# Four graph layers in fp32: a quarter of each symmetric product mirrored by VectorE square transposes and SBUF-to-SBUF transfers instead of TensorE, h^T of layer 3 turned from h, and a new plan

## The chip, the cores and the metric

The kernel runs on one core of one Trainium2 chip. The metric is the device time of one execution in microseconds; the figure that counts is the median of several runs. The engines of the core are TensorE (PE in the profile; its weight loads are listed apart as PEld), VectorE (DVE), ScalarE (ACT) and GpSimd (POOL). SyncE (SP) does no arithmetic here: it issues DMA transfers, one after the other, in the order in which they stand in the program. Everything is computed in fp32.

## What is computed

There are 16 graphs of 1024 nodes with 128 features, and four layers in a row, each of the form x = x + layer(relu(layernorm(x))). The layers that matter here are 0 and 3, which build a 1024 x 1024 symmetric matrix; layers 1 and 2 are given in a line each.

```python
# layer 0, three times (i = 0, 1, 2)
h = h @ W[i] + b[i]
nh = h / max(norm(h), EPS)
cos = einsum('bij,bkj->bik', nh, nh)          # symmetric, 1024 x 1024
h = einsum('bpq,bqc->bpc', adj * cos, h)
h = relu(h)                                    # not after the last one

# layer 1: y = relu(((1 + eps) * h + adj^T h) @ W1 + b1) @ W2 + b2
# layer 2: softmax of tanh(s1 + s2) over the neighbours, times h @ W

# layer 3
h = einsum('bnf,of->bno', x, W_w) + W_b
e = einsum('bil,bkl->bik', h @ A, h)
e = e + swapaxes(e, 1, 2)                      # symmetric, 1024 x 1024
att = softmax(where(adj > 0, e, 0), axis=1) * adj
h_prime = relu(einsum('bij,bjk->bik', att, h))
# then three sigmoid gates from x and h_prime, and a tanh
```

## The kernel before

**Tiles.** A graph is a "batch" in the code. Its 1024 nodes are eight blocks (`NB`) of 128 (`P`), the partitions of the memory. x and h stand as 128 x 1024, block after block along the free dimension. A row j of a square is 128 nodes against all 1024, worked in two halves (`HALVES`, s = 0 and 1) of four blocks[...].

**A square.** `row_of_square` (line 582) makes half a row of the symmetric product in PSUM. Blocks on or above the diagonal are multiplied (L587). Blocks below it are mirrored: the block above the diagonal was copied out of PSUM by ACT in `keep_above` (L609) into a buffer `above` with places for 22 blocks (`PLACE`), and PE transposes it into the row (L597), one instruction per block. There are 36 multiplied and 28 transposed blocks in a square. Of these 28, sixteen are the lower left quarter: rows 4 to 7, half 0. `layer0` has three squares a batch; each half row is multiplied by the norm and the adjacency on DVE (L740, tile `ew`) and then used by PE as an operand of the sum over nodes (`acc`, L620 in the first two, L631 in the third). `layer3` has one: DVE masks the half row (L921, tile `e`), takes the row's maximum (L930), ACT exponentiates (L934), DVE multiplies by the adjacency (L941), and PE accumulates (L620).

**h in layer 3.** Two forms of it are wanted. The transposed one, `hT`, is an operand of the square; before the change it is a product of its own on PE, `ph` (L463, two of 512 columns a batch, beside `pg` for the other operand `gT`), with the bias added by ACT. The plain one, `h`, comes from the products `psP` (L453) and a DVE addition (L909). In it a block is 131 columns wide (`E3`), since three gate columns stand beside each block.

**Loads.** The transposed adjacency of a batch, eight tiles `adjT` of 128 x 1024, is fetched from HBM as 32 x 32 squares put in transposed place, in four transfers a tile (L673), and each square is then turned by DVE (L681) and summed by ACT (L684). The plain rows, `adjL`, come later for layer 1 (L654), and x by L646. All are issued by SP. Sixteen adjT slots are two batches; a slot comes free in layer 3, after L941 of the old tile.

**What sets the order.** The program first lists every operation with a cost in microseconds, what it reads and what it writes, for all batches. `Plan.order` then simulates the five queues (PE, DVE, ACT, POOL, DMA) with these costs and fixed latencies, and places one operation after the other: of those that can start earliest on an engine, the one with the smallest rank. The rank is a due time of the batch (`PERIOD`, `LAST`) less the work that follows, less an entry of the table `LEADS` for its kind ("02 DVE ew" is the kind ew on DVE in the third square of layer 0). Buffers are slots of pools (`POOLS`); `KINDS` limits how many a kind may hold, and how many younger batches may. Operations of up to three batches are mixed. The result is one fixed order for each engine. On the chip each engine, and SP, takes its instructions strictly in this order and waits by semaphores.

Of the kernel before, what the change touches and what calls it, by code (L numbers as in the profile page):

```python
# [14 lines left out]
P = 128  # L15
N = 1024
NB = N // P
D = 128
# [200 lines left out]
def tile_adj_preln(  # L219
# [96 lines left out]
    for load_it in first:  # L316
# [8 lines left out]
    bg = const.tile([D, 1], F32, name="bg")  # L325


    POOLS = {"adjT": 16, "adjL": 4, "x": 3, "big": 16, "above": 2, "bank": 8, "small": 25, "row": 5}
    KINDS = {
        "adjT": ("adjT", 16, 16), "adjL": ("adjL", 4, 4), "x": ("x", 3, 3), "w4": ("big", 13, 13),  # L330
        "chunk": ("big", 12, 4), "above": ("above", 2, 1), "ps": ("bank", 6, 4), "acc": ("bank", 6, 4),
        "small": ("small", 19, 7), "row": ("row", 3, 2),
    }
    PERIOD, LAST, AHEAD, WINDOW = 74.0, 9.0, 2, 0.02

    LEADS = {
        "0 ACT hT": -82.5, "0 ACT hn": 118.5, "0 DVE hn": 4.5, "0 DVE mv": -23.5, "0 DVE nb": -70,
        "0 DVE st": -22.5, "0 PE ps": -2.5, "0 POOL rstd": -10, "00 ACT hT": -39.5, "00 ACT hTn": -130.5,
        "00 ACT sq": -51, "00 DMA params": -55.5, "00 DVE ew": -9.5, "00 DVE h": -17.5, "00 DVE params": 4,
        "00 PE acc0": -148, "00 PE params": -1, "00 PE ps": -43.5, "00 PE psP": -14.5, "00 PE sq": 11.5,  # L340
        "00 POOL rn": 17.5, "01 ACT above": -5, "01 ACT hTn": -2.5, "01 ACT sq": -2.5, "01 DVE ew": 130.5,
        "01 DVE h": 4, "01 DVE ss": 1.5, "01 PE ps": -315, "01 PE psP": 37, "01 PE sq": -2, "01 POOL rn": 0.5,
        "02 ACT above": 9, "02 ACT hTn": 20, "02 ACT sq": -24, "02 DVE ew": 70.5, "02 DVE h": 54,
        "02 DVE ss": -52, "02 DVE x": 50.5, "02 PE acc0": 20.5, "02 PE ps": 6.5, "02 PE psP": 193,
        "02 PE sq": 127.5, "02 POOL rn": 15.5, "1 ACT g": 0.5, "1 ACT y1": 7, "1 DMA adjL": -303.5,
        "1 DVE adjL": -206.5, "1 DVE hn": -5, "1 DVE mv": -39.5, "1 DVE nb": 77.5, "1 DVE st": 8.5,
        "1 DVE x": 89.5, "1 PE acc1": -17.5, "1 PE py": -17, "1 PE py2": 2.5, "1 POOL rstd": -43.5,
        "2 ACT e2": -22, "2 ACT h": -71, "2 ACT hfl": -9, "2 ACT hn": 11.5, "2 ACT hnT": 196, "2 DVE alone": -1,
        "2 DVE e2": 7.5, "2 DVE h": -40, "2 DVE hn": 12.5, "2 DVE hrow": -4.5, "2 DVE mv": 20,
        "2 DVE rden": -64, "2 DVE st": -9.5, "2 DVE x": 101.5, "2 PE p1": -7.5, "2 PE pf": -35.5,  # L350
        "2 PE ps": -227, "2 PE psP": -292, "3 ACT above": -242.5, "3 ACT e3": -38.5, "3 ACT gT": 62.5,
        "3 ACT gate": -13.5, "3 ACT h3T": -65.5, "3 ACT hn": 24, "3 ACT hnT": 18, "3 ACT hp": 17,
        "3 ACT hs": -65.5, "3 DMA z": 17, "3 DVE e3": -116, "3 DVE gate": 6.5, "3 DVE hn": 69, "3 DVE mv": 14.5,
        "3 DVE nb": 254, "3 DVE st": 66, "3 DVE sum": -74, "3 DVE top": 3, "3 DVE z": 29.5, "3 PE acc3": -12,
        "3 PE ph": 198.5, "3 PE ps": 49.5, "3 PE psN": -172.5, "3 PE psP": 6, "3 POOL rstd": 59.5,
        "3 POOL z": -22.5, "T ACT adjT": 127.5, "T DMA adjT": -128.5, "T DVE adjT": -231.5, "x DMA x": 9,
    }
    plan = Plan(POOLS, KINDS, lambda b: min(b * PERIOD, (B - 2) * PERIOD + LAST), AHEAD, WINDOW, LEADS)
    now = [0, ""]
# [7 lines left out]
    def pe(us, reads, writes, fn):  # L367
        return op("PE", us, reads, writes, fn)
# [13 lines left out]
    def ps(name):  # L382
        return Buf("ps", [P, HALF], name)
# [11 lines left out]
        return Buf("row", [P, D], name)  # L395


    MM_BLOCK = 0.222
    MM = 4 * P / 2400
    TR = 0.109  # L400
    TINY = 0.09
    STT = 0.262

# [10 lines left out]
    def blk(b, lo, hi, w=D):  # L414

        return (b, lo * w, hi * w)

    def cols(t, c, w=D):
        return t[:, c * w : c * w + P]

    def span(t, lo, hi):
        return t[:, lo * P : hi * P]
# [12 lines left out]
    def power(dst, src):  # L435
        pool_op(1.64, [src], [dst], lambda: nc.gpsimd.tensor_tensor(dst.t, src.t, mhalf, op=ALU.pow))  # L436

    def flip(src, lo, hi, dst):


        def emit():
            for c in range(lo, hi):
                nc.tensor.transpose(cols(dst.t, c - lo), cols(src.t, c), ident)  # L443

        pe((hi - lo) * TR, [blk(src, lo, hi)], [dst], emit)

    def project(srcT, lo, hi, w, dst):

# [27 lines left out]

        act(S((hi - lo) * P, bias is not None, accum is not None), [src], w, emit)

    def flipped(src, name, func=AF.Copy, accum=None):

        dst = w4(name)
        for s, (lo, hi) in enumerate(HALVES):
            p = ps(f"ps_{name}_{s}")
            flip(src, lo, hi, p)
            evict(p, dst, lo, hi, func, accum=(accum, s) if accum else None)
        return dst

# [82 lines left out]

    PLACE = {(0, 1): 16, (0, 2): 17, (0, 3): 18, (1, 2): 19, (1, 3): 20, (2, 3): 21}
    for r in range(4):
        for c in range(4, NB):
            PLACE[r, c] = r * 4 + c - 4
    PLACE.update({(4, 5): 16, (4, 6): 17, (4, 7): 18, (5, 6): 19, (5, 7): 20, (6, 7): 21})

    def row_of_square(k, j, s, leftT, rightT, above):

        lo, hi = HALVES[s]
        dst = ps(f"sq_{k}_{j}_{s}")
        first = max(lo, j)
        if first < hi:
            pe(
                (hi - first) * MM, [blk(leftT, j, j + 1), blk(rightT, first, hi)], [dst],
                lambda: nc.tensor.matmul(  # L587
                    dst.t[:, (first - lo) * P :], cols(leftT.t, j), span(rightT.t, first, hi), start=True, stop=True
                ),
            )  # L590
        n = min(hi, j) - lo
        if n > 0:
            at = [PLACE[r, j] for r in range(lo, lo + n)]

            def mirrored():
                for r, p in enumerate(at):
                    nc.tensor.transpose(cols(dst.t, r), cols(above.t, p), ident)  # L597

            pe(n * TR, [blk(above, p, p + 1) for p in at], [dst], mirrored)
        return dst  # L600

    def keep_above(dst, j, s, above):
        lo, hi = HALVES[s]
        first = max(lo, j + 1)
        if first < hi:
            p = PLACE[j, first]
            act(
                S((hi - first) * P), [dst], [blk(above, p, p + hi - first)],
                lambda: nc.scalar.copy(span(above.t, p, p + hi - first), dst.t[:, (first - lo) * P :]),  # L609
            )  # L610

    def above_of(k):
        return Buf("above", [P, 22 * P], f"above_{k}")

    def accumulate(acc, h, at, w, ew, j):

# [72 lines left out]
    def layer0(b, xt, aT, prepared):  # L689
# [4 lines left out]
        for i in range(3):  # L694
# [34 lines left out]
            dve(TINY, [ss], [ss], lambda ss=ss: nc.vector.tensor_scalar_max(ss.t, ss.t, NORM_EPS * NORM_EPS))  # L729
            rn = small(f"rn_{k}", NB)  # L730
            power(rn, ss)
            above = above_of(k)
            acc = [bank(f"acc0_{k}_{s}") for s in range(2)]
            for j in range(NB):
                ew = chunk(f"ew_{k}_{j}")
                for s, (lo, hi) in enumerate(HALVES):
                    pc = row_of_square(k, j, s, hTn, hTn, above)
                    o = dve(
                        V(HALF, True), [pc, rn, blk(aT[j], lo, hi)], [blk(ew, lo, hi)],
                        lambda pc=pc, ew=ew, rn=rn, j=j, lo=lo, hi=hi: nc.vector.scalar_tensor_tensor(  # L740
                            span(ew.t, lo, hi), pc.t, rn.t[:, j : j + 1], span(aT[j].t, lo, hi),
                            op0=ALU.mult, op1=ALU.mult,
                        ),
                    )
                    keep_above(pc, j, s, above)
                if prepared is None and j == 3:
                    prepared = prepare(o)
                if i < 2:
                    accumulate(acc, h, j, D, ew, j)
                else:  # L750
                    accumulate_nodes(acc, HALVES, h, j, D, D, ew)
# [137 lines left out]
    def layer3(b, xt, aT):  # L889
# [2 lines left out]
        hn = layernorm(k, xt)  # L892
        hnT = flipped(hn, f"hnT_{k}", AF.Relu)
        relu(hn)
        hT, gT = w4(f"h3T_{b}"), w4(f"gT_{b}")
        for s, (lo, hi) in enumerate(HALVES):
            for dst, w, v, name in ((hT, w3e[:, 0:D], wb3col, "ph"), (gT, wg, bg, "pg")):
                p = ps(f"{name}_{b}_{s}")
                wide(p, w, hnT, lo, hi)
                evict(p, dst, lo, hi, AF.Identity, v)  # L900

        h = w4(f"h_{k}")
        for lo, hi in THIRDS:
# [6 lines left out]
                    by_block(h.t[:, lo * E3 : hi * E3], E3, n), by_block(pp.t, E3, n), per_feature(b3e, n)  # L910
                ),
            )
        above = above_of(k)
        acc = [bank(f"acc3_{b}_{s}") for s in range(2)]
        for j in range(NB):
            e = chunk(f"e3_{b}_{j}")
            for s, (lo, hi) in enumerate(HALVES):
                p = row_of_square(k, j, s, gT, hT, above)
                dve(
                    V(HALF), [blk(aT[j], lo, hi), p], [blk(e, lo, hi)],  # L920
                    lambda e=e, p=p, j=j, lo=lo, hi=hi: nc.vector.scalar_tensor_tensor(  # L921
                        span(e.t, lo, hi), span(aT[j].t, lo, hi), 0.0, p.t, op0=ALU.is_gt, op1=ALU.mult
                    ),
                )
                keep_above(p, j, s, above)
            top = small(f"top_{b}_{j}", 1)
            tot = small(f"sum_{b}_{j}", 1)
            dve(
# [192 lines left out]
```

## Time and profile before

| | |
|---|---|
| median of 3 runs | 2551.03 us (2550.04 to 2552.56) |
| profiled execution: its time | 2549.91 us |
| profiled execution: span of the trace | 2548.1 us |
| mean granted TensorE clock | 0.995 |
| SP queue (q1) | 567552 packets, 142.65 MB, 29.6% of the 16 DMA engines' span |
| PE matmuls L597 (mirrored blocks) | 1792, idle before them 4.9 us |
| DVE L740 (ew) | 768, mean 741 ns |

The profile is of one execution, so sums are made against its 2549.91 us; the trace's span is 1.8 us shorter than that. In rows by line, "busy" is the time that the group kept its engine busy, "mean" is how long one instruction took from start to end, and after the bar stands the idle time of the engine just before them, with what ended it. Instructions of one engine overlap at their ends, so the pitch from one to the next is less than the mean. An engine's idle time costs something only where the chain of work runs through it.

### The profile page before, as it was taken

What the parts mean: (1) busy time and instruction counts of PE and PEld (TensorE: products, weight loads), DVE (VectorE), ACT (ScalarE), POOL (GpSimd) and SP (SyncE); (2) the same over time, 40 slices, a digit from 0 to 9 for tenths busy, and PEclk for the clock granted to TensorE, in tenths of its full rate; (3) what the DMA queues carried; (4) which work ended last, traced back from release to release, by engine and by line L of the source; (5) the groups of instructions that cost most, each with busy time, mean ns of one, the idle gap of its engine ahead of it and who ended that gap; (6) DMA issues with size and microseconds to landing.
All of it is one profiled execution on the core that took longest, in us unless ns stands there. A gap on an engine that the chain in (4) does not pass through costs nothing.

```text
span 2548.1 us, 35510 instructions
## 1 busy us (share of the span) xinstructions
PE 2500.2 (98%) x12714; PEld 1674.1 (66%) x12714; DVE 2003.7 (79%) x5070; ACT 1384.7 (54%) x2609; POOL 215.3 (8%) x134
## 2 busy tenths in 40 slices
PE   7999999999999999999999999999999999999996
PEld 4567576775667666676666767657676666765763
DVE  6658979787787968879687796877878778796777
ACT  4426575644646556455654656447464564554365
POOL 1001000101101010010100101010010100100000
PEclk9999999999999999999999999999999999999998
DMA  9320706133070430604216052340614306042100
GB/s 138 68 67 4 146 1 101 49 52 98 1 124 26 59 91 11 133 7 67 83 26 123 1 84 66 46 104 1 116 34 59 91 8 122 21 59 75 30 12 17
DMA packets 588641, 154.32 MB, mean 61 GB/s; under 512 B 537520, under 2 KB 572080, under 8 KB 588464
## 3 DMA queue, kind: packets, MB, share of 16 engines
q1 hardware_dynamic: 567552, 142.65, 29.6%
q10 hardware_dynamic: 20912, 9.40, 1.4%
q8 instruction: 100, 1.64, 0.3%
q14 instruction: 77, 0.63, 0.1%
HBM read 143.61 MB, written 8.39 MB: 60 GB/s over the span
## 4 chain that ended last, share of the span: by engine, by line
PE 91%; DVE 4%; ACT 2%; DMA 1%; SPq 1%; issue 1%; POOLq 0%; POOL 0%; ACTq 0%; DVEq 0%
PE acc L620 33%; PE acc L631 18%; PE sq L587 17%; PE sq L597 7%; PE psP L453 5%; PE py L463 2%; PE py L792 2%; PE ps_hTn L443 1%; PE ph L463 1%; PE ps_hnT L443 1%; PE pg L463 1%; PE psN L453 1%; SPq L673 1%; DVE e L921 1%; DVE top L930 1%; ACT e L934 1%
## 5 line engine op out<-in xcount | busy, mean ns | idle before, releaser
L740 DVE SCALAR_TENSOR_TENSOR ew<-sq,rn,adjT 128x512 f32<-128x512 f32 x768 | 555.0, 741 | 133.9 <-PE sq L597 84.4
L609 ACT COPY above<-sq 128x512 f32<-128x512 f32 (+3 forms) x640 | 285.2, 455 | 491.6 <-DVE ew L740 431.1
L620 PE MATMUL acc<-ew,h 128*128 128x512 f32 x1024 | 498.4, 597 | 1.6 <-DVE ew L740 1.5
L587 PE MATMUL sq<-hTn 128*128 128x512 f32 (+3 forms) x1152 | 452.2, 489 | 2.4 <-ACT hTn L475 2.4
L597 PEld LDWEIGHTS sq<-ident,above 128*128 128x128 f32 x1792 | 226.5, 141 | 156.9 <-issue 108.3
L597 PE MATMUL sq<-ident,above 128*128 128x128 f32 x1792 | 299.8, 273 | 4.9 <-ACT above L609 4.9
L620 PEld LDWEIGHTS acc<-ew,h 128*128 128x128 f32 x1024 | 177.2, 191 | 147.0 <-issue 100.2
L587 PEld LDWEIGHTS sq<-hTn 128*128 128x128 f32 x1152 | 189.3, 191 | 121.2 <-issue 84.6
L631 PEld LDWEIGHTS acc<-h,ew 128*128 128x128 f32 x2048 | 244.1, 192 | 31.7 <-issue 14.4
L631 PEld LDWEIGHTS acc<-h,e 128*128 128x128 f32 x2048 | 239.9, 193 | 30.3 <-issue 27.1
L631 PE MATMUL acc<-h,ew 128*128 128x128 f32 x2048 | 251.5, 275 | 0.3 <-DVE ew L740 0.3
L631 PE MATMUL acc<-h,e 128*128 128x129 f32 x2048 | 241.1, 276 | 2.5 <-DVE e L862 2.5
L934 ACT ACTIVATE e<-e,top 128x1024 f32<-128x1024 f32 x128 | 146.9, 1148 | 171.9 <-DVE top L930 166.5
L620 PE MATMUL acc<-e,hs 128*128 128x512 f32 x512 | 235.7, 596 | 1.5 <-DVE e L941 1.5
L620 PE MATMUL acc<-adjL,hn 128*128 128x512 f32 x512 | 236.8, 593 | 0.3 <-ACT hn L567 0.2
L862 DVE SCALAR_TENSOR_TENSOR e<-adjT,e 128x512 f32<-128x512 f32 x256 | 165.2, 686 | 64.0 <-ACT e L858 63.8
L436 POOL TENSOR_TENSOR rstd<-ve,mhalf 128x8 f32<-128x8 f32 x64 | 104.8, 1637 | 1096.0 <-DVE ve L528 1092.6
L684 ACT ACTIVATE adjT<-adjT 128x1024 f32<-128x1024 f32 x128 | 135.3, 1057 | 95.5 <-DVE adjT L681 78.5
L921 DVE SCALAR_TENSOR_TENSOR e<-adjT,sq 128x512 f32<-128x512 f32 x256 | 170.5, 675 | 6.5 <-PE sq L587 6.5
L941 DVE TENSOR_TENSOR e<-e,adjT 128x512 f32<-128x512 f32 x256 | 167.3, 679 | 0.0
L681 DVE STREAM_TRANSPOSE adjT<-adjT 128x1024 f32<-128x1024 f32 x128 | 155.8, 1229 | 8.8 <-DMA adjT<-in_adj_dram 4.6
L620 PEld LDWEIGHTS acc<-adjL,hn 128*128 128x128 f32 x512 | 93.8, 190 | 101.4 <-issue 88.6
(121 smaller groups left out, 3260.8 us busy)
## 6 DMA issues: line engine op xcount, KB each, us to landing
adjT<-in_adj_dram SPq DMA_DIRECT2D x512, 128.0 KB, 3.9
adjL<-in_adj_dram SPq DMA_DIRECT2D x128, 512.0 KB, 4.0
x<-in_x_dram SPq DMA_DIRECT2D x16, 512.0 KB, 5.1
out_dram<-z ACTq DMA_DIRECT2D x16, 512.0 KB, 5.6
b<-in_L_gnn_b_dram ACTq DMA_DIRECT2D x4, 64.0 KB, 4.5
w<-in_L_gnn_W_dram ACTq DMA_DIRECT2D x2, 128.0 KB, 3.9
w<-in_L_gnn_W_dram ACTq DMA_DIRECT2D x3, 64.0 KB, 3.5
w2e<-in_L_gnn_W_dram ACTq DMA_DIRECT2D x1, 64.0 KB, 2.7
```

The costliest lines, as they stand in the source:

```text
L453: nc.tensor.matmul(dst.t[:, (c - lo) * n : (c - lo + 1) * n], cols(srcT.t, c), w, start=True, stop=True)
L587: lambda: nc.tensor.matmul(dst.t[:, (first - lo) * P :], cols(leftT.t, j), span(rightT.t, first, hi), start=True, stop=True),
L597: nc.tensor.transpose(cols(dst.t, r), cols(above.t, p), ident)
L609: lambda: nc.scalar.copy(span(above.t, p, p + hi - first), dst.t[:, (first - lo) * P :]),
L620: lambda s=s, lo=lo, hi=hi: nc.tensor.matmul(acc[s].t, cols(h.t, at, w), span(ew.t, lo, hi), start=(j == 0), stop=(j == NB - 1)),
L631: nc.tensor.matmul(a.t[:, (c - lo) * n : (c - lo + 1) * n], cols(ew.t, c), h.t[:, j * w : j * w + n], start=(j == 0 and c == lo), stop=(j ...
L681: dve(V(N), [t], [t], lambda t=t: nc.vector.transpose(t.t, t.t), True)
L740: lambda pc=pc, ew=ew, rn=rn, j=j, lo=lo, hi=hi: nc.vector.scalar_tensor_tensor(span(ew.t, lo, hi), pc.t, rn.t[:, j : j + 1], span(aT[j].t ...
L862: lambda e=e, j=j, lo=lo, hi=hi: nc.vector.scalar_tensor_tensor(span(e.t, lo, hi), span(aT[j].t, lo, hi), 0.0, span(e.t, lo, hi), op0=ALU. ...
L921: lambda e=e, p=p, j=j, lo=lo, hi=hi: nc.vector.scalar_tensor_tensor(span(e.t, lo, hi), span(aT[j].t, lo, hi), 0.0, p.t, op0=ALU.is_gt, op ...
L934: lambda e=e, top=top, tot=tot: nc.scalar.activation(e.t[:, 0:N], e.t[:, 0:N], AF.Exp, bias=top.t, accum_out=tot.t),
L941: lambda e=e, j=j, lo=lo, hi=hi: nc.vector.tensor_mul(span(e.t, lo, hi), span(e.t, lo, hi), span(aT[j].t, lo, hi)),
```

## The change

Three things are changed, and the plan's numbers.

1. In batches 1 to 13 (`FAR`) the lower left quarter of each square is not transposed by PE. When half 1 of rows 0 to 3 has been multiplied, DVE turns each 32 x 32 square of it, from PSUM into `above` (`keep`), where ACT copied it before. After rows 1 and 3, SP sends two rows' worth from `above` to a new buffer `got` (`send`): 16 transfers within SBUF, one for each pair of partition groups of 32, which move the squares to their transposed places, 128 bytes a piece. In rows 4 to 7 the DVE operation (ew in layer 0, the mask in layer 3) reads `got` for half 0 where it read PSUM. There is one `got`. The rest of a square is as before, and batches 0, 14 and 15 keep PE's transposes throughout.
2. In layer 3 of all batches `hT` is turned from `h` by PE transposes (`flipped`, with blocks 131 wide) and copied out by ACT; the product `ph` is gone.
3. `PLACE` is numbered anew.
4. The pools, the limits, the due times, PE's costs and the table `LEADS` are replaced, so that the fixed order of all engines is a new one. There is one more adjL slot, and three fewer of the large buffers.

```diff
-    POOLS = {"adjT": 16, "adjL": 4, "x": 3, "big": 16, "above": 2, "bank": 8, "small": 25, "row": 5}
+    POOLS = {"adjT": 16, "adjL": 5, "x": 3, "big": 13, "above": 2, "got": 1, "bank": 8, "small": 30, "row": 4}
     KINDS = {
-        "adjT": ("adjT", 16, 16), "adjL": ("adjL", 4, 4), "x": ("x", 3, 3), "w4": ("big", 13, 13),
-        "chunk": ("big", 12, 4), "above": ("above", 2, 1), "ps": ("bank", 6, 4), "acc": ("bank", 6, 4),
-        "small": ("small", 19, 7), "row": ("row", 3, 2),
+        "adjT": ("adjT", 16, 16), "adjL": ("adjL", 5, 5), "x": ("x", 3, 3), "w4": ("big", 13, 5),
+        "chunk": ("big", 10, 8), "above": ("above", 2, 1), "got": ("got", 1, 1), "ps": ("bank", 7, 5),
+        "acc": ("bank", 8, 5), "small": ("small", 12, 6), "row": ("row", 2, 2),
     }
-    PERIOD, LAST, AHEAD, WINDOW = 74.0, 9.0, 2, 0.02
+    PERIOD, LAST, AHEAD, WINDOW = 61.0, 2.0, 2, 0.02
 
     LEADS = {
...
     }
...
-    MM_BLOCK = 0.222
-    MM = 4 * P / 2400
-    TR = 0.109
+    MM_BLOCK = 0.2235
+    MM = 0.2155
+    TR = 0.1097
+
+    FAR = range(1, B - 2)
...
-    def flip(src, lo, hi, dst):
+    def flip(src, lo, hi, dst, w=D):
 
 
         def emit():
             for c in range(lo, hi):
-                nc.tensor.transpose(cols(dst.t, c - lo), cols(src.t, c), ident)
-
-        pe((hi - lo) * TR, [blk(src, lo, hi)], [dst], emit)
+                nc.tensor.transpose(cols(dst.t, c - lo), cols(src.t, c, w), ident)
+
+        pe((hi - lo) * TR, [blk(src, lo, hi, w)], [dst], emit)
...
-    def flipped(src, name, func=AF.Copy, accum=None):
+    def flipped(src, name, func=AF.Copy, accum=None, w=D):
...
-            flip(src, lo, hi, p)
+            flip(src, lo, hi, p, w)
...
-    PLACE = {(0, 1): 16, (0, 2): 17, (0, 3): 18, (1, 2): 19, (1, 3): 20, (2, 3): 21}
-    for r in range(4):
-        for c in range(4, NB):
-            PLACE[r, c] = r * 4 + c - 4
-    PLACE.update({(4, 5): 16, (4, 6): 17, (4, 7): 18, (5, 6): 19, (5, 7): 20, (6, 7): 21})
...
-
-        lo, hi = HALVES[s]
-        dst = ps(f"sq_{k}_{j}_{s}")
-        first = max(lo, j)
...
-    def keep_above(dst, j, s, above):
-        lo, hi = HALVES[s]
-        first = max(lo, j + 1)
-        if first < hi:
-            p = PLACE[j, first]
-            act(
-                S((hi - first) * P), [dst], [blk(above, p, p + hi - first)],
-                lambda: nc.scalar.copy(span(above.t, p, p + hi - first), dst.t[:, (first - lo) * P :]),
-            )
...
+    PLACE = {(0, 1): 0, (0, 2): 1, (0, 3): 2, (1, 2): 3, (1, 3): 4, (2, 3): 5}
+    PLACE.update({(r + 4, c + 4): p for (r, c), p in PLACE.items()})
+    PLACE.update({(r, c): 6 + r * 4 + c - 4 for r in range(4) for c in range(4, NB)})
+    QUARTER = NB // 2
+
+    class Square:
+
+
+        def __init__(self, k, leftT, rightT, by_dma):
+            self.k, self.leftT, self.rightT, self.by_dma = k, leftT, rightT, by_dma
+            self.above = Buf("above", [P, 22 * P], f"above_{k}")
+
+            self.got = Buf("got", [P, QUARTER * HALF], f"got_{k}") if by_dma else None
+
+        def row(self, j, s):
+
+            lo, hi = HALVES[s]
+            if self.by_dma and j >= QUARTER and s == 0:
+                q = j - QUARTER
+                return self.got, lambda: self.got.t.rearrange("p (r c d) -> p c r d", r=QUARTER, d=P)[:, q]
+            leftT, rightT, above = self.leftT, self.rightT, self.above
...
+            return dst, lambda: by_block(dst.t, D, 4)
+
+        def keep(self, j, s, read):
+
+            lo, hi = HALVES[s]
+            if self.by_dma and j < QUARTER and s == 1:
+                p, above = PLACE[j, lo], self.above
+                dve(
+                    V(HALF), [read], [blk(above, p, p + 4)],
+                    lambda: nc.vector.transpose(span(above.t, p, p + 4), read.t),
+                )
+                if j % 2:
+                    self.send(j - 1, j + 1)
+                return
+            first = max(lo, j + 1)
+            if first < hi:
+                p, above = PLACE[j, first], self.above
+                act(
+                    S((hi - first) * P), [read], [blk(above, p, p + hi - first)],
+                    lambda: nc.scalar.copy(span(above.t, p, p + hi - first), read.t[:, (first - lo) * P :]),
+                )
+
+        def send(self, lo, hi):
+
+            above, got = self.above, self.got
+            at, end = PLACE[lo, QUARTER], PLACE[hi - 1, NB - 1] + 1
+
+            def squares_to_places():
+                for a in range(P // SQ):
+                    for g in range(P // SQ):
+                        src = span(above.t, at, end)[a * SQ : (a + 1) * SQ]
+                        dst = span(got.t, lo * 4, hi * 4)[g * SQ : (g + 1) * SQ]
+                        with nc.allow_non_contiguous_dma(reason="squares"):
+                            nc.sync.dma_start(
+                                dst.rearrange("p (b a i) -> p b a i", a=P // SQ, i=SQ)[:, :, a],
+                                src.rearrange("p (b g i) -> p b g i", g=P // SQ, i=SQ)[:, :, g],
+                            )
+
+            op("DMA", 1.9 * (hi - lo), [blk(above, at, end)], [blk(got, lo * 4, hi * 4)], squares_to_places)
...
-            above = above_of(k)
+            square = Square(k, hTn, hTn, b in FAR)
...
-                    pc = row_of_square(k, j, s, hTn, hTn, above)
+                    pc, view = square.row(j, s)
...
-                        lambda pc=pc, ew=ew, rn=rn, j=j, lo=lo, hi=hi: nc.vector.scalar_tensor_tensor(
-                            span(ew.t, lo, hi), pc.t, rn.t[:, j : j + 1], span(aT[j].t, lo, hi),
-                            op0=ALU.mult, op1=ALU.mult,
+                        lambda view=view, ew=ew, rn=rn, j=j, lo=lo, hi=hi: nc.vector.scalar_tensor_tensor(
+                            by_block(span(ew.t, lo, hi), D, 4), view(), rn.t[:, j : j + 1],
+                            by_block(span(aT[j].t, lo, hi), D, 4), op0=ALU.mult, op1=ALU.mult,
                         ),
+                        pc is square.got,
                     )
-                    keep_above(pc, j, s, above)
+                    square.keep(j, s, pc)
...
-        hT, gT = w4(f"h3T_{b}"), w4(f"gT_{b}")
+        gT = w4(f"gT_{b}")
         for s, (lo, hi) in enumerate(HALVES):
-            for dst, w, v, name in ((hT, w3e[:, 0:D], wb3col, "ph"), (gT, wg, bg, "pg")):
-                p = ps(f"{name}_{b}_{s}")
-                wide(p, w, hnT, lo, hi)
-                evict(p, dst, lo, hi, AF.Identity, v)
+            p = ps(f"pg_{b}_{s}")
+            wide(p, wg, hnT, lo, hi)
+            evict(p, gT, lo, hi, AF.Identity, bg)
...
-        above = above_of(k)
+        hT = flipped(h, f"h3T_{b}", w=E3)
+        square = Square(k, gT, hT, b in FAR)
...
-                p = row_of_square(k, j, s, gT, hT, above)
+                p, view = square.row(j, s)
                 dve(
                     V(HALF), [blk(aT[j], lo, hi), p], [blk(e, lo, hi)],
-                    lambda e=e, p=p, j=j, lo=lo, hi=hi: nc.vector.scalar_tensor_tensor(
-                        span(e.t, lo, hi), span(aT[j].t, lo, hi), 0.0, p.t, op0=ALU.is_gt, op1=ALU.mult
+                    lambda e=e, view=view, j=j, lo=lo, hi=hi: nc.vector.scalar_tensor_tensor(
+                        by_block(span(e.t, lo, hi), D, 4), by_block(span(aT[j].t, lo, hi), D, 4), 0.0, view(),
+                        op0=ALU.is_gt, op1=ALU.mult,
                     ),
+                    p is square.got,
                 )
-                keep_above(p, j, s, above)
+                square.keep(j, s, p)
```

## The prediction

> **What bounds the kernel now.** I read the page's busy shares first, then the chain that ended last, then a table by stretches over one period of the steady part, then the rows of the operations that the edit touches, and last the sync engine's (SP's) queue in order of time.
>
> ```profile
> PE 2500.2 (98%) x12714; PEld 1674.1 (66%) x12714; DVE 2003.7 (79%) x5070; ACT 1384.7 (54%) x2609; POOL 215.3 (8%) x134
> ...
> PE 91%; DVE 4%; ACT 2%; DMA 1%; SPq 1%; issue 1%; POOLq 0%; POOL 0%; ACTq 0%; DVEq 0%
> ```
>
> TensorE (PE) is busy 98% of the span and carries 91% of the chain that ended last; VectorE (DVE) carries 4%. To see whether that holds within a stage, I took one period. SP's queue in order of time gives it (loads of the transposed adjacency, and of its rows):
>
> ```profile
> 701.25 37.69 SPq L673 DMA_DIRECT2D adjT<-in_adj_dram  x32
> 746.20 20.71 SPq L654 DMA_DIRECT2D adjL<-in_adj_dram  x8
> 768.47 0.38 SPq L646 DMA_DIRECT2D x<-in_x_dram  x1
> 856.51 37.69 SPq L673 DMA_DIRECT2D adjT<-in_adj_dram  x32
> ```
>
> One batch takes 856.51 - 701.25 = 155.26 us. Cut into three stretches (start:end, length, then busy us of PE, PEld, DVE, ACT, POOL, then clock, DMA share and GB/s):
>
> ```profile
> 694.00:751.00 57.00, 56.83 (x284) 37.40 (x283) 55.87 (x110) 30.19 (x63) 3.27 (x2) 1.00 0.63 86
> 751.00:838.00 87.00, 87.00 (x459) 59.40 (x458) 58.78 (x185) 47.82 (x84) 10.08 (x6) 1.00 0.17 53
> 838.00:849.30 11.30, 11.30 (x58) 7.44 (x57) 10.22 (x22) 8.32 (x18) 0.00 (x0) 1.00 0.00 1
> sum 155.30, PE 155.13 PEld 104.23 DVE 124.87 ACT 86.33 POOL 13.35; mean PE 51.71 PEld 34.74 DVE 41.62 ACT 28.78 POOL 4.45
> ```
>
> PE has 0.17 us free in a period: the period is its work. DVE has 30 us free, but almost none of it between 694 and 751, where layer 3 of one batch lies over the last square of layer 0 of the next. The rows that the edit touches:
>
> ```profile
> L597 PE MATMUL sq<-ident,above 128*128 128x128 f32 x1792 | 299.8, 273 | 4.9 <-ACT above L609 4.9
> L463 PE MATMUL ph<-hnT,w3e 128*128 128x512 f32 x64 | 30.3, 594 | 0.2 <-ACT hnT L475 0.2
> L681 DVE STREAM_TRANSPOSE adjT<-adjT 128x1024 f32<-128x1024 f32 x128 | 155.8, 1229 | 8.8 <-DMA adjT<-in_adj_dram 4.6
> L921 DVE SCALAR_TENSOR_TENSOR e<-adjT,sq 128x512 f32<-128x512 f32 x256 | 170.5, 675 | 6.5 <-PE sq L587 6.5
> L609 ACT COPY above<-sq 128x512 f32<-128x512 f32 x256 | 149.7, 586 | 65.5 <-DVE ew L740 57.0 <-DVE e L921 6.8
> ```
>
> The means are latencies of pipelined instructions; what counts is the pitch, which the chain shows as pieces in order of time:
>
> ```profile
> 715.93 0.44 PE sq L597 x4
> ...
> 727.34 9.44 PE acc L620 x22
> ...
> 833.35 1.72 PE ph L463 x4
> ```
>
> Four mirroring transposes take 0.44 us, so 0.11 us each; ph takes 1.72 us a batch.
>
> **What the Trainium skill says.** "VectorE: DVE Perf Modes", The three transpose paths: DVE transposes 32x32 blocks only, not a whole 128x128 block. So the DMA half of the mirror is needed, and L681 is the nearest priced operation (1229 ns for 1024 columns). "DMA: Bandwidth & Descriptors", Anatomy of one DMA: a semaphore wait happens on the issuing sequencer before dispatch, not in the DMA engines. The trace agrees: SP's queue stood 1304.3 us at L673 waiting for DVE L941. A send placed behind a load whose slot is not free stands with it. The same page, Why small descriptors are slow (HBM only), says SBUF-to-SBUF transfers do not suffer the small-packet penalty; no transfer of the kernel before is of this kind, so I use it only to say that the send need not be dearer per packet than the load from HBM.
>
> **Part by part.**
>
> 1. Mirror on PE. `FAR` is batches 1 to 13. Each has four squares (three in layer 0, one in layer 3), and in each the 4x4 blocks of rows 4 to 7, left half, are no longer transposed on PE: 16 x 0.11 = 1.75 us a square, 7.0 us a batch, 13 x 7.0 = 91.3 us. With the chain on PE all of it is on the path.
>
> 2. h^T turned from h. Two ph products (1.72 us) go, eight transposes (8 x 0.11 = 0.88 us) come: -0.84 us a batch, in all 16 batches -13.5 us. The ACT evictions are as many as before. h^T now waits for h (DVE L909), one stage later; at 838 the trace shows other PE work to stand in, so I cost that at nothing; uncovered it would be about 1 us a batch.
>
> PE sum: -104.8 us; the period becomes 155.26 - 7.86 = 147.4 us.
>
> 3. DVE. 16 transposes of 128x512 a batch. L681 has a pitch of 1.14 to 1.17 us for 1024 columns in the order of time, and L921, which reads PSUM at 512 columns, has a pitch of 0.60: I take 0.62 us, bounds 0.60 (L921's pitch) and 0.68 (its mean), so 16 x 0.62 = 9.9 us a batch. The 16 products that read `got` instead of PSUM I take as unchanged: L862, with both operands in SBUF, is 686 ns against L921's 675. DVE comes to 124.9 + 9.9 = 135 us of 147.4, 92%.
>
> 4. ACT loses 16 copies of 586 ns, 9.4 us a batch, to 77 us. Off the path, worth nothing itself.
>
> 5. Sends. Two a square, eight a batch, 16 DMAs each. A DMA moves 32 partitions x 8 pieces of 128 bytes, so a send is 4096 packets, exactly as many as a load of one adjT tile. Eight tiles took 37.69 us: 4.7 us a tile. Issue: the cheapest adjT issue took 311 ns, the x load 379, the first four adjT issues 2.23 us together (0.56 each). So 16 issues cost 16 x 0.31 = 5.0 to 16 x 0.56 = 8.9 us, and the last lands 2.4 us (the shortest landing) to 3.9 us (the median) later: 7.4 to 12.8 us from the turned row 3 to data; I take 9. In all 104 sends add 425,984 packets to 567,552. At the same price per packet the queue's share goes from 29.6% to 52%: bandwidth is there on average.
>
> What hides those 9 us? Row 4's left half waits for `got`. Before it PE can do, of the same square, the right halves of rows 4 to 7 (2.2 us products, 0.7 us transposes), their accumulations (4 x 0.86) and row 3's (1.7): 8 us; and other batches' work. So the wait is nearly covered by the square alone. The queue behind it is the danger: DVE takes its instructions in order, so when the product that reads `got` stands, everything behind it stands, and PE soon after.
>
> 6. Where covers run short I take 0.5 us of PE idle a square, 2 us a batch, 26 us in 13. Ends: the bounds are 0 (covered as worked out) and 3.7 us a square (12.8 - 9 more than the middle, nothing in front), 194 us; a gain below nothing is excluded, since nothing else gets earlier by it. The table of due times is new too; inside the steady part it can give at most the 0.17 us a period that PE has free. At the ends PE idles 18 us in the first 78 and 24 us in the last 98 (a sum of the windows 2450 to 2500 and 2500 to 2548); I leave both as they are, with +-8 us.
>
> Sum against the profiled execution (span 2548.1, 2549.91 with what lies around it): 2549.9 - 104.8 + 26 = 2471. The median of three runs is 1.1 us higher, so **2472 us**.
>
> **Rivals.**
>
> A. All hidden: the new plan covers every send. 2551 - 104.8 = 2446. For it: PE lost only 0.17 us a period before. Against: DVE at 92% leaves less to shift.
>
> B. DVE becomes the bound where it is full. In 694 to 751 it is 98% busy; two squares fall there, 8 x 0.62 = 5 us more, while PE's saving there (3.5 us) becomes idle. If it were all so, the period would change by +5 + 3.5 - 7.86 = +0.6 us, no change. But PE's filler (acc of layer 1, the 9.44 us piece at 727) needs little of DVE and can be moved in from the other 98 us; at half, 2551 - 104.8 + 13 x 4.2 = 2501, up to 2546.
>
> C. The other side: sends stand behind loads on SP's one queue. The loads of adjT go out exactly while layer 3 and the last square of layer 0 run (701 to 739), and 8 tiles and 4 sends need 12 x 4.7 = 56 us of a stretch of 57. A send with one load and one send ahead is 9.4 us late, beyond what the square covers. It decides from 104.8 / 13 = 8.1 us of PE idle a batch. With two such squares and half of it covered by other work, 9.4 us plus the 2 us of part 6: 2551 - 104.8 + 13 x 11.4 = 2594; milder, 2560. Against it: the order on SP is fixed ahead, and the loads have time, since the tile turned at 749 is first read near 795.
>
> **Numbers.** 0.2% (5 us) is what a measurement here can tell from none. Forecast (own range 2450 to 2500) 0.48; A 0.12; B above 2500 but faster 0.15; a standoff 0.03; C 0.22. Hence faster 0.75, same 0.03, slower 0.22. The range takes A, the forecast, B and the edge of C: 2438 to 2565, with about 2 in 10 left out.
>
> **What would show it.** PE instructions: 12714 - 832 - 64 + 128 = 11946; DVE 5070 + 208 = 5278; ACT 2609 - 208 = 2401; the SP queue near 993,500 packets. The period of the x loads near 149.4 us with PE idle about 2 us in it. A: idle below 0.5. B: DVE full from end to end of a stretch while PE's waits name DVE products that read PSUM. C: DVE's waits name DMA got, several us each, with SP's loads in front of them. The forecast falls if PE idles more than 8 us a period, or if the sends take far more than 9 us with the queue empty.

## The result and the profile after

The changed kernel takes 2924.03 us (median of 4 runs, 2921.45 to 2925.47) against 2551.8 us of the kernel before beside it: ratio 1.1458, 95% interval 1.1438 to 1.1478. It is 372 us slower; a faster one was forecast. Lines are numbered as in the changed kernel from here on (L740 is now L784, L921 is L966, L597 is L616, L609 is L638; in the runs e5 and e9 below some move on by one to four). The first part of the page:

```profile
PE 2529.6 (87%) x11946; PEld 1667.5 (57%) x11946; DVE 2128.1 (73%) x5278; ACT 1285.6 (44%) x2401; POOL 214.7 (7%) x134
```

The instruction counts are those that the prediction gave: TensorE (PE) has 768 instructions fewer. Yet it is busy 29 us longer than before, and idle 391 us in a span of 2921.1 us, where it was idle 48. The queue of SyncE (SP) in order of time shows one batch, from one load of x to the next:

```profile
948.02 0.54 SPq L690 DMA_DIRECT2D x<-in_x_dram  x1
982.02 20.87 SPq L652 DMA_DIRECT2D got<-above  x32
1003.00 6.98 SPq L717 DMA_DIRECT2D adjT<-in_adj_dram  x8
1014.61 21.10 SPq L652 DMA_DIRECT2D got<-above  x32
1035.82 6.10 SPq L717 DMA_DIRECT2D adjT<-in_adj_dram  x8
1042.02 2.38 SPq L698 DMA_DIRECT2D adjL<-in_adj_dram  x2
1044.49 10.39 SPq L652 DMA_DIRECT2D got<-above  x16
1054.98 0.54 SPq L698 DMA_DIRECT2D adjL<-in_adj_dram  x1
1055.62 14.67 SPq L717 DMA_DIRECT2D adjT<-in_adj_dram  x16
1071.89 10.39 SPq L652 DMA_DIRECT2D got<-above  x16
1082.38 2.54 SPq L698 DMA_DIRECT2D adjL<-in_adj_dram  x5
1107.33 22.90 SPq L652 DMA_DIRECT2D got<-above  x32
1130.36 0.52 SPq L690 DMA_DIRECT2D x<-in_x_dram  x1
```

The period is 182.34 us, 27.1 more than before. A send of 16 transfers keeps SP's queue for 10.4 us, eight of them for 83 us, and the loads of adjT and adjL, which stood together before, stand between them. The windows of this period and of the stretch of its first two sends (columns as before):

```profile
948.02:1130.36 182.34, 158.60 (x734) 104.26 (x734) 134.52 (x332) 78.61 (x147) 13.35 (x8) 0.92 0.39 76
```
```profile
982.00:1003.00 21.00, 18.08 (x100) 12.56 (x98) 15.51 (x24) 6.60 (x14) 0.00 (x0) 1.00 0.29 47
```

PE is idle 23.7 us of the period and its clock is 0.92. While two sends are issued the DMA engines are busy 29%: the transfers wait to be issued, not to be moved. Moving was even cheaper than the prediction took it: SP's queue used 35.9% of the DMA engines' span where 52% of a shorter one were expected. The rows by line:

```profile
L784 DVE SCALAR_TENSOR_TENSOR ew<-got,rn,adjT 128x512 f32<-128x512 f32 x156 | 111.9, 745 | 237.3 <-DMA got<-above 225.4 <-PE acc L664 10.6 <-PE acc L675 0.2
...
L966 DVE SCALAR_TENSOR_TENSOR e<-adjT,got 128x512 f32<-128x512 f32 x52 | 34.4, 688 | 99.4 <-DMA got<-above 99.4
```
```profile
L628 DVE STREAM_TRANSPOSE above<-sq 128x512 f32<-128x512 f32 x208 | 146.1, 708 | 5.2 <-PE sq L606 5.1
```

VectorE (DVE) stands 324.8 us before the operations that read `got`, 6.2 us for each of the 52 squares. The transposes themselves (L628) cost 0.70 us of DVE each and wait for nothing. SP's own waits, and one place in order of time, first DVE and then PE:

```profile
SPq L652 <- DVE above L628: 518.5, 20, 59.3
SPq L652 <- DVE z L502: 272.0, 22, 25.4
```
```profile
1004.38 0.75 DVE L784 SCALAR_TENSOR_TENSOR ew<-got,rn,adjT 128x512 f32<-128x512 f32 x1 [5.53 <-DMA got<-above]
...
1106.60 0.71 DVE L628 STREAM_TRANSPOSE above<-sq 128x512 f32<-128x512 f32 x1
```
```profile
999.06 1.02 PE L606 MATMUL sq<-hTn 128*128 128x512 f32 x2
1005.19 1.22 PE L675 MATMUL acc<-h,ew 128*128 128x128 f32 x4 [5.11 <-DVE ew L784]
```

Two things go wrong on SP. A square comes late, DVE stands for it in its fixed order, and PE stands for DVE (5.11 us at 1000). And SP itself stands at a send until DVE has turned the squares, with loads behind it. The second line of SP's waits is of the same kind, though the profile names z: the send at 1107.33 starts when the turn at 1106.60 has ended, at 1107.31. The experiments weigh these.

Over the whole span the largest part of PE's idle time comes by one step more:

```profile
PE sq L616 <- ACT above L638: 132.2, 21, 8.1
PE acc L675 <- DVE ew L784: 75.6, 16, 7.6
PE acc L664 <- DVE ew L784: 58.3, 20, 5.8
PE acc L664 <- DMA adjL<-in_adj_dram: 34.6, 11, 4.7
PE sq L616 <- DMA adjT<-in_adj_dram: 26.7, 4, 6.7
```

The plan puts ACT's copy of a half row (L638) behind DVE's operation on it, so when DVE stands, the copy comes late, and with it PE's transposes of the blocks that it still mirrors (L616). In e1 below, without the transfers, that wait is 0.7 us.

### The profile page after: what moved, and what is told of

The parts are those of the page before. It is cut to its first block, busy times and chain, and to the rows that moved or that the text cites. A ratio compares the mean times of both kernels' runs of the same rounds, so it can differ in the third digit from the quotient of the medians.

```text
span 2921.1 us, 35953 instructions
## 1 busy us (share of the span) xinstructions
PE 2529.6 (87%) x11946; PEld 1667.5 (57%) x11946; DVE 2128.1 (73%) x5278; ACT 1285.6 (44%) x2401; POOL 214.7 (7%) x134
## 3 DMA queue, kind: packets, MB, share of 16 engines
q1 hardware_dynamic: 1020160, 197.28, 35.9%
## 5 line engine op out<-in xcount | busy, mean ns | idle before, releaser
L784 DVE SCALAR_TENSOR_TENSOR ew<-sq,rn,adjT 128x512 f32<-128x512 f32 x612 | 440.3, 743 | 163.2 <-PE sq L606 71.6
L638 ACT COPY above<-sq 128x384 f32<-128x384 f32 (+3 forms) x432 | 168.4, 393 | 727.8 <-DVE ew L784 562.6
L675 PE MATMUL acc<-h,ew 128*128 128x128 f32 x2048 | 277.7, 290 | 75.6 <-DVE ew L784 75.6
L675 PEld LDWEIGHTS acc<-h,ew 128*128 128x128 f32 x2048 | 266.2, 205 | 118.9 <-DVE ew L784 90.7
L616 PE MATMUL sq<-ident,above 128*128 128x128 f32 x960 | 184.7, 286 | 158.9 <-ACT above L638 132.2
L664 PE MATMUL acc<-adjL,hn 128*128 128x512 f32 x512 | 268.4, 664 | 35.5 <-DMA adjL<-in_adj_dram 34.6
L784 DVE SCALAR_TENSOR_TENSOR ew<-got,rn,adjT 128x512 f32<-128x512 f32 x156 | 111.9, 745 | 237.3 <-DMA got<-above 225.4
L616 PEld LDWEIGHTS sq<-ident,above 128*128 128x128 f32 x960 | 132.1, 149 | 266.6 <-ACT above L638 175.2
L675 PEld LDWEIGHTS acc<-h,e 128*128 128x128 f32 x2048 | 260.6, 207 | 30.4 <-DVE e L907 17.9
L675 PE MATMUL acc<-h,e 128*128 128x129 f32 x2048 | 264.3, 291 | 12.9 <-DVE e L907 12.9
L441 POOL TENSOR_TENSOR rstd<-ve,mhalf 128x8 f32<-128x8 f32 x64 | 104.8, 1637 | 2135.8 <-DVE ve L533 2135.8
L725 DVE STREAM_TRANSPOSE adjT<-adjT 128x1024 f32<-128x1024 f32 x128 | 156.1, 1227 | 31.9 <-DMA adjT<-in_adj_dram 31.9
```

What stands on the lines that cost most here:

```text
L638: lambda: nc.scalar.copy(span(above.t, p, p + hi - first), read.t[:, (first - lo) * P :]),
L664: lambda s=s, lo=lo, hi=hi: nc.tensor.matmul(acc[s].t, cols(h.t, at, w), span(ew.t, lo, hi), start=(j == 0), stop=(j == NB - 1)),
L675: nc.tensor.matmul(a.t[:, (c - lo) * n : (c - lo + 1) * n], cols(ew.t, c), h.t[:, j * w : j * w + n], start=(j == 0 and c == lo), stop=(j ...
L725: dve(V(N), [t], [t], lambda t=t: nc.vector.transpose(t.t, t.t), True)
L784: lambda view=view, ew=ew, rn=rn, j=j, lo=lo, hi=hi: nc.vector.scalar_tensor_tensor(by_block(span(ew.t, lo, hi), D, 4), view(), rn.t[:, j ...
```

## The experiments

The runs are called e1 to e11 by the start of their labels.

**What the sends cost, taken apart.** Three kernels keep the exact order of the changed kernel on every engine; what is emitted for a send differs, and rows 4 to 7 read `above`.

```diff
-                return self.got, lambda: self.got.t.rearrange("p (r c d) -> p c r d", r=QUARTER, d=P)[:, q]
+                return self.got, lambda: span(self.above.t, 6, 22).rearrange("p (r c d) -> p c r d", r=QUARTER, d=P)[:, q]
...
-            op("DMA", 1.9 * (hi - lo), [blk(above, at, end)], [blk(got, lo * 4, hi * 4)], squares_to_places)
+            op("DMA", 1.9 * (hi - lo), [blk(above, at, end)], [blk(got, lo * 4, hi * 4)], lambda: None)
```

> The changed kernel in its exact order on every engine, but the sends issue nothing, and rows 4 to 7 read the squares that VectorE turned where they lie, so the blocks stay in their old places: the movement of the squares is left out. Theory 'late sends': the got waits (22 us a batch) and what hangs on them go, TensorE is back at its work of 147 us a batch and at full clock; 2440 to 2490 us, granted clock above 0.98. Rival 'VectorE and the new order': the time stays within 60 us of 2924, with VectorE waiting on TensorE and the reverse where got stood before.

2451.08 us, ratio 0.9604 (0.9588 to 0.9620), clock 0.993. One period by windows:

```profile
788.17:934.79 146.62, 146.62 (x737) 97.84 (x736) 133.43 (x333) 78.40 (x148) 13.35 (x8) 1.00 0.33 65
```

PE is busy all of the period, at full clock, with DVE at 91%. So the saving on PE is real and the new order is a good one as long as nothing is sent; all of the loss comes with the sends. With the sends issued and unread (the second pair of lines above left as in the changed kernel):

> As e1_no_send, but the sends are issued as in the changed kernel; nothing reads what they bring. Theory 'late sends' in the form that the wait for their data costs: as e1 within 30 us. In the form that SyncE's queue is occupied by the 16 issues of each send (10.4 us each, 83 us a batch) and the loads behind them come late: clearly above e1, by 100 us or more, with waits for adjL and adjT.

2772.56 us, ratio 1.0865 (1.0843 to 1.0887). Leaving `got` unread takes away 151 of the 473 us between e1 and the changed kernel; 321 us come without anybody reading it. Its waits name loads that in e1 hardly appear (27.3 us for the first):

```profile
DVE adjL L820 <- DMA adjL<-in_adj_dram: 209.1, 50, 12.7
...
PE acc L664 <- DMA adjL<-in_adj_dram: 147.6, 22, 10.5
DVE st L522 <- DMA x<-in_x_dram: 65.2, 14, 6.1
```

Are these loads late because the issues fill the queue, or because SP stands at a send for DVE? The same with each transfer taking a constant square:

```diff
-                        src = span(above.t, at, end)[a * SQ : (a + 1) * SQ]
+                        src = ident[a * SQ : (a + 1) * SQ, g * SQ : (g + 1) * SQ]
...
-                                src.rearrange("p (b g i) -> p b g i", g=P // SQ, i=SQ)[:, :, g],
+                                src[:, None, :].to_broadcast([SQ, 4 * (hi - lo), SQ]),
```

> As e2_send_unread (16 issues a send at the same places of SyncE's queue, rows 4 to 7 reading the squares where VectorE left them, got unread), but each transfer takes a constant square, so that SyncE needs not stand for VectorE's turns. The movement of the right squares is left out. If the 83 us of issues a batch by themselves make the loads late, it stays within 60 us of e2 (2772). If it is SyncE standing at the sends with loads behind it, the time falls to 2450 to 2550, near e1 (2451).

2567.75 us, ratio 1.0063 (1.0045 to 1.0082), between the two expectations. An issue takes the same here (609 ns by the median), so the issues alone cost 117 us over e1, and SP standing for the turned squares 205 us more. The wait for adjL at L820 is 88.1 us here. Taken away in this order, the 473 us are 117 (occupied queue), 205 (queue standing) and 151 (late squares). The causes can hide one another, so that another order may share the sum otherwise: in the changed kernel itself PE's waits name loads for only 34.6 and 26.7 us. One rival was not tried: there is one `got`, so a send also waits until the last square has been read (the send at 1014.61 starts when the read that began at 1013.83 has ended, at 1014.58), and a second one might have brought some squares earlier.

**What an issue costs.** One send of 16 transfers a square in place of two:

```diff
+            first = PLACE[0, QUARTER]
+
             def squares_to_places():
+                if lo == 0:
+                    return
...
-                        src = span(above.t, at, end)[a * SQ : (a + 1) * SQ]
-                        dst = span(got.t, lo * 4, hi * 4)[g * SQ : (g + 1) * SQ]
+                        src = span(above.t, first, end)[a * SQ : (a + 1) * SQ]
+                        dst = span(got.t, 0, hi * 4)[g * SQ : (g + 1) * SQ]
```

> The changed kernel, but the two sends of a square are one, issued where the second was: 16 transfers of twice the pieces (32x16x32 for 32x8x32), the same bytes and packets, half the transfers. If an issue costs SyncE a fixed 0.65 us whatever its pieces, a square takes 10.4 us of its queue in place of 20.8, the loads come earlier and the time falls by 100 to 300 us, to 2620 to 2820. If it is the pieces or the packets that cost, each issue takes 1.3 us, data come later than before (the first half no longer goes ahead), and the time is 2900 or more.

2656.65 us, ratio 1.0417 (1.0344 to 1.0489), inside the first forecast. The issues (min/median/max in ns), in the changed kernel and then here:

```profile
L652 SPq DMA_DIRECT2D got<-above x1664: 585/609/2423, 71.9 to 2651.0; - x185
```
```profile
L656 SPq DMA_DIRECT2D got<-above x832: 585/627/2032, 82.3 to 2392.7; - x167
```

Twice the pieces, nearly the same price: it is the number of transfers that costs. Half of them on ScalarE's queue (`nc.sync if a < 2 else nc.scalar`):

> The changed kernel, but half of each send's 16 transfers are issued by ScalarE's queue, the other half by SyncE's as before. If the issue is a serial cost of the issuing queue, SyncE's occupancy halves (5.2 us a send) and the time falls below 2800, less what ScalarE (44% busy) loses by 42 us of issues a batch and by standing at VectorE's turns. If both queues feed one serial generator of transfers, the pitch of an issue doubles to 1.3 us on each and the time is 2920 or more.

2886.98 us, ratio 1.1320 (1.1276 to 1.1364). An issue costs 626 ns on ScalarE's queue and 609 on SP's, so the queues issue beside each other and no shared generator shows; SP's 16 issues became 8 in 5.2 us. DVE's waits for `got` are nearly gone, 18.9 us where they were 324.8. The forecast of less than 2800 failed all the same, since ScalarE now stands for its own issues: its exponentials and copies wait behind them, for instance 142.8 us in all before L997, and PE waits 170.9 us for its copies (L616). All sends by GpSimd (`nc.gpsimd.dma_start`):

> The changed kernel, but all sends are issued by GpSimd, which is 93% idle. SyncE then has loads only: the loss that e2_send_unread showed by late loads goes. If GpSimd issues at 0.65 us or faster: 2500 to 2650, what is left being the wait for got. If it writes its transfers' descriptors slower than that (over 1.3 us a transfer), got comes later than now and the time is above 2924.

2809.68 us, ratio 1.1017 (1.0976 to 1.1057), between both cases. GpSimd issues at the same price:

```profile
L652 POOL DMA_DIRECT2D got<-above x1664: 582/582/775, 74.1 to 2533.9; - x185
```

SP's loads are together again, and the wait for adjL at L820 is back at 26.2 us. But 166.8 us of waits for `got` stay at ew, and GpSimd's reciprocal roots come behind the sends: DVE's normalised rows wait 98.0 us for them where they waited 4.4, and ScalarE waits 126.9 us at L572 for these rows where it waited 31.9. So e7 is 359 us above e1 with its loads in time; it exchanged one loss for another and does not measure the late squares alone.

**The plan.** Its cost for a send is 3.8 us where SP's queue is kept for 10.4. The true cost, with the same table of due times (`1.9 * (hi - lo)` became `5.2 * (hi - lo)`):

> The changed kernel with the plan's cost of a send raised from 3.8 to the 10.4 us that the trace shows for its 16 issues; the same instructions in another order. Theory 'late sends because the plan took them for short': the order moves work in front of the reads of got, got waits fall below half of 325 us in all, and the time falls to 2550 to 2750. Rival 'nothing can hide them, or the order is bad anyway': stays above 2850.

3084.83 us, ratio 1.2089 (1.2064 to 1.2113): worse. DVE's waits for `got` fell from 324.8 to 185.6 us, not below half, and other waits of PE grew, as that for DVE's normalised rows (L448, 75.6 us where it was 2.3). It seems that a right cost under a table made for a wrong one gives another bad order; this alone decides nothing. Therefore one send a square at its cost, 10.0, and `LEADS`, `PERIOD` and `LAST` searched anew by the end time of the plan:

```diff
-                if j % 2:
-                    self.send(j - 1, j + 1)
+                if j == QUARTER - 1:
+                    self.send(0, QUARTER)
...
-            op("DMA", 1.9 * (hi - lo), [blk(above, at, end)], [blk(got, lo * 4, hi * 4)], squares_to_places)
+            op("DMA", 10.0, [blk(above, at, end)], [blk(got, lo * 4, hi * 4)], squares_to_places)
```

> The changed kernel with one send of 16 transfers a square in place of two, its cost in the plan at 10 us as e5_one_send showed it, and the due times searched anew for that. Theory: what the change lost is transfers whose issue the plan took for 3.8 us; with half of them and an order that knows it, got waits and late loads shrink and the time falls to 2500 to 2570, near or below the kernel before. Rival: late squares cannot be hidden at this issue rate: above 2620, as e5 (2657).

2584.81 us, ratio 1.0132 (1.0116 to 1.0147), between the theory and its rival, and still slower than before. The waits at ew for `got` are down from 225.4 to 47.9 us, but PE idles 152 us, 88.2 of them in twelve waits of some 7 us each for an ew that had stood for `got`:

```profile
PE acc L665 <- DVE ew L785: 88.2, 12, 8.0
```

PE's busy time fell by 69 us against the kernel before, its idle time rose by 104. In this order the transfers are not hidden well enough to pay; whether a longer search would do it stays open.

**h^T turned from h, alone.** The kernel before with this part only, and its old table:

> The kernel before with one part of the change alone: h^T of layer 3 turned from h, the plan's numbers of before. By the sum, 13.5 us of TensorE work less: 2538, ratio 0.995. Rival: h^T comes one stage later and the stall eats it: ratio 0.999 or above.

2617.11 us, ratio 1.0255 (1.0240 to 1.0271): 67 us slower, with less work on PE. The same with the table searched anew:

> As e4_turned_only (the kernel before with h^T of layer 3 turned from h, every mirrored block on TensorE), with a table of due times searched anew for just these operations. Theory: the 67 us that e4 lost came from an order made for other operations, not from h^T coming a stage later; so the time falls below the kernel before, by the 13.5 us of TensorE work and perhaps some idle at the ends: 2515 to 2540, ratio below 0.997. Rival: the later h^T costs in any order: 2550 or more.

2541.94 us, ratio 0.9963 (0.9950 to 0.9975), 2 us above the forecast but faster than both kernels, by a little. PE is busy 2487.6 us, 12.6 less than before. As a control the kernel before itself, with a table searched in the same way:

> The kernel before with nothing changed but its due times, searched anew as for e8_turned_new. If e8's gain (9 us) came from the 13.5 us of TensorE work that h^T turned from h saves, this stays within 5 us of the kernel before, ratio 0.998 to 1.002. If it came from the new search, this is as fast as e8, ratio 0.996 or less.

2557.23 us, ratio 1.0023 (1.0015 to 1.0031), no gain, even a small loss of 6 us. So the new search by itself does not bring e8's gain, which speaks for the part's own, and e4's loss went with the old order. Each table is the outcome of one search, though, and how far two searches for the same operations differ was not measured.

## Why the prediction was wrong

**PE sum (parts 1 and 2): right.** The period was put at 147.4 us if nothing stalls; e1 has 146.62. It runs 99 us faster than the kernel before where 104.8 were worked out.

**DVE (part 3): right.** 135 us a batch were predicted, 134.5 measured; a transpose costs 0.70 us of busy time, just above the upper bound of 0.68, which changed nothing. Rival B falls with e1: PE full at 91% of DVE.

**h^T (part 2): right in size, wrong in "costed at nothing".** PE's busy time in e8 is 12.6 us below the kernel before (8.3 below e11), where 13.5 were worked out. But one stage later in an order made for the earlier stage cost 67 us (e4); only a new order brought a gain.

**Sends (parts 5 and 6): the step that failed** is the price of a send on SP's queue, and with it the stall that was costed at 2 us of PE a batch. "A send is 4096 packets, exactly as many as a load of one adjT tile" led me to price the queue by what the DMA engines take, 4.7 us. SP's queue is kept by issues: 16 x 0.65 = 10.4 us. The bound of 0.31 to 0.56 us an issue came from the cheapest and the first four adjT issues; the median of all 512 in the trace of before was there to be read:

```profile
L673 SPq DMA_DIRECT2D adjT<-in_adj_dram x512: 311/576/2473, 1.9 to 2295.0; - x171
```

The 4.7 us were misread as well: of the 37.69 us for eight tiles SP stood about 15 for free slots, so that their 32 issues took some 22 us, 0.7 us each. One send alone, 10.4 us and 1.9 to land, is 12.3 us, still inside my bounds of 7.4 to 12.8. What they left out is the queue: with two squares under way, sends come back to back for 21 us, and 8 loads and 4 sends need 22 + 4 x 10.4 = 64 us of issuing alone in the stretch of 57 us for which I had counted 56, before SP stands for a slot or a turned square.

**Stalls (part 6).** Part 5 named the way, DVE standing for `got` and PE soon after, but I sized it at 0.5 us of PE a square, at most 3.7, in all 26 us for 13 batches. DVE waits 6.2 us a square, and PE idles 23.7 us a batch instead of 2. That SP itself would stand for the turned squares, with loads behind it, is in no term of the sum. (Two slips in the sums changed nothing: 52 x 3.7 is 192 and not 194, and the full case of B comes to 2559 and not 2546.)

**The clock, not in the sum at all.** PE's busy time a batch is 158.6 us where the same work takes 146.6 in e1: 12 us more at a clock of 0.92. So the measured period of 182.3 splits into 146.6 of work, 12.0 by the clock and 23.7 of idle, where the forecast had 147.4 + 2.

**Rival C was the right mechanism at 0.22, and too cheap:** it put the time at 2560 to 2594. It named loads and sends on one queue, but saw sends held up by loads. The larger part, taken away in the order above, is the reverse: loads behind sends (117 us) that themselves stand for DVE (205 us by e10 and e2). "The loads have time", my argument against it, was made from adjT alone; in e2 it is adjL (209.1 us at L820) and x (65.2) that come late, more than adjT (54.7).

## What to carry to other kernels

Price a transfer twice: what it takes of the DMA engines, and what its issue takes of the queue that issues it, counted in transfers and not in bytes; sixteen small ones can cost more than the work they replace. A transfer that waits for a computation does not belong ahead of prefetches on one in-order queue, because all of them then wait for that computation. And where the order is fixed by a cost model, one stage moved can be worth more than the operation itself (67 us against 13.5 in e4): remake the order before judging the edit.

## What the runs showed of the hardware

**The issue of a strided transfer costs about 0.6 us, for 512 pieces as for 256,** 582 to 627 ns by the median: on SP 609 for 256 pieces of 128 bytes and 627 for 512, on ScalarE 626 and on GpSimd 582 for 256. In the kernel before, the x load took 379 ns and adjL 328. The Trainium skill, "DMA: Bandwidth & Descriptors", Issuing engines are not separate DMA queues, calls the time to initiate a transfer usually small relative to the transfer itself. Here it was not: the 16 issues of a send took 10.4 us and the last landed 1.9 us later, at 29% busy DMA engines; the measurement decides. On SP's queue a transfer also brought 16 packets more than its pieces: 1020160 packets, 452608 more than before, for 1664 x 256 = 425984 pieces; in e5, with half the transfers for the same pieces, 439296 more.

**Idle on PE is paid twice.** Kernels with the same 11946 PE instructions, each from its profiled execution:

| | span less PE busy, us | granted clock | PE busy, us |
|---|---|---|---|
| e1 | 59 | 0.993 | 2390 |
| e10 | 133 | 0.978 | 2433 |
| e9 | 152 | 0.969 | 2431 |
| e5 | 204 | 0.969 | 2458 |
| e2 | 287 | 0.945 | 2484 |
| e7 | 308 | 0.948 | 2497 |
| e6 | 346 | 0.943 | 2543 |
| after | 391 | 0.934 | 2530 |
| e3 | 487 | 0.919 | 2595 |

The skill's "TensorE: Matmul & The Clock Gate", Why this matters for your kernels, warns that idle gaps of over some 3 us drop the clock. These traces agree for the long gaps: right after the gap of 5.11 us, which ended at 1005.19, the clock is 0.56 for 6.8 us, and 0.88 over the longer stretch,

```profile
1005.20:1012.00 6.80, 6.80 (x31) 6.09 (x32) 5.68 (x9) 1.88 (x3) 0.00 (x0) 0.56 0.91 137
...
1003.00:1036.00 33.00, 27.69 (x116) 18.31 (x116) 22.79 (x56) 8.25 (x18) 1.64 (x1) 0.88 0.42 65
```

while in e1's period, where PE has no gap, it is 1.00. Each trace keeps a record of the granted clock, which is 1.0 or 0.5 at any time. Counted over all 13 traces, gaps of PE that began at 1.0 were followed by a stretch of 0.5 (begun within 3.4 us of the gap's end) in all 228 cases of 4 us or longer, in 65 of 72 from 3 to 4 us, in 56 of 99 from 2 to 3 us and in 23 of 307 from 0.3 to 2 us. So gaps of 2 to 3 us are not safe here; the measurement decides.
